# Attention block on one core: values' halves set between contexts and scores, the scores' second part set behind the next query half, and round-trip turns at the attention's end no longer tied to the last norm

## The chip, the cores and the metric

The kernel runs on one core of a Trainium2 chip. A core has five engines with instruction streams of their own: TensorE (PE in the profile; its weight loads are listed as PEld), VectorE (DVE), ScalarE (ACT), GpSimd (POOL) and SyncE (SP), which issues most transfers. The metric is the device time of one execution in microseconds (us), lower is better; a kernel's time is the median of its runs.

## The reference, cut to what matters

A pre-norm transformer block in float32 on 2048 tokens of width 1024 (the file's shapes, with the batch dimension left out here):

```python
x = x + attention(layernorm(x), wq, bq, wk, bk, wv, bv)
x = x + ffn(layernorm(x), w1, w2, w3)

# attention: 32 heads of 32; each token attends over its own heads
q, k, v = (h @ w.T + b).reshape(S, 32, 32)
scores  = einsum("shd,std->sht", q, k) / sqrt(32)
context = einsum("sht,std->shd", softmax(scores), v)

# ffn: the weights go through a 4-bit rounding and back (NF4, blocks of 64)
h = silu(x @ dq(w1).T) * (x @ dq(w2).T)
y = h @ dq(w3).T
```

The attention mixes the heads of one token, not tokens, so it falls into 2048 tiny 32x32 products. `dq` is the weights' round trip: divide a block by its largest magnitude, round to one of 16 levels, multiply back.

## The kernel before

**Tiles.** The 2048 tokens are 16 tiles of 128 (`NT = 16`). All of it stands in `forward`; what follows is its fast half (`if fast:`), which is the one that runs. PE takes its instructions in the order in which the program writes them (`manual_schedule` for TensorE). The other engines' orders are made by the framework's scheduler from the dependences, so a piece of work that is written late can be placed early on DVE, ACT, POOL or SP, if nothing holds it back.

**One tile of attention** passes through these helpers (lines of the kernel before):

- `prepare(i)` normalises the tile's input `xt` into `xn` on ACT and POOL (L592, L579, L585). `split(i)` transposes `xn` on PE (L618) and writes a high part `xh` on ACT (L620) and a low part `xl` on DVE (L621).
- `Q(i, n)`, `K(i, n)`, `V(i, n)`, each for a half n = 0, 1 of the output columns: 16 matmuls of 128x128 by 128x512 into one PSUM bank `pj` (`project`, L648), then a transposing copy out of the bank on DVE (L665 into `qd` or `kd`, L678 into `vd`), with the bias after the second half.
- `S(i, part)`: the scores of half of the tile's tokens, 64 products of 32x32 (L696; the trace shows them as 128 matmuls and 128 weight loads) into the buffer `at`. After part 1 comes the softmax: maximum (L733), subtraction (L735), `Exp` on ACT (L741), a transpose into `prT` (L743).
- `G(i, part)`: the contexts, again 64 tiny products (L700) from `prT` and `vd` into `at`. After part 1 DVE divides by the sums (L758, L760 into `pw`), transposes (L768), adds the residual (L771), SP stores the result and loads the input of tile i + 3, and ACT and POOL normalise it (`norm`, L578 to L585).
- `keep(i)` transposes the normalised result on PE (L511), copies it out on ACT (L512) and stores it for the FFN, with sums and differences made on DVE (L527).

**Buffers that order the work.** `at` takes four of the eight PSUM banks and exists once: scores and contexts take turns in it, so `S(i, 0)` must wait until `G(i-1, 1)` has been read by `pw` (L760). The other four banks turn among `pj`, the transposes `pt` and the weights' transposes `ptw`. `qd`, `kd`, `vd`, `prT` and `xn` have one buffer each.

**The round trip.** The FFN's weights are rounded in the background by a generator. `advance(n)` grants it n * 10/17 turns; a turn is one rounding band (an ACT activation L299 and a DVE step L303 or L305), or the maxima of the next chunk. `flush(1)` writes one half of a finished chunk's transposes to PE (L219), which ACT copies out (L220). Where `held["behind"]` is set, `turn()` tells the scheduler to place the turn's instructions behind the instruction named there.

**The order of one turn of the loop** over tiles i = 3 to 14, before: Q(i,0), Q(i,1), keep(i-2), K(i,0), G(i-1,0), K(i,1), G(i-1,1), V(i,0), S(i,0), V(i,1), split(i+1), S(i,1). Tile 2 has a shorter turn, and tile 15 has no split. In front of the loop stand V(1,0), S(1,0), V(1,1), S(1,1), K(2,1), keep(0), split(3).

**The end of the attention.** After the loop, `plain_block` gives the first eight quads of FFN matmuls (four 128x512 products each, 3.6 us a quad in the trace) in pieces; keep(14), G(15,0), G(15,1) and keep(15) stand between the pieces. After G(15,1) the kernel sets `held["behind"]` to the last instruction of tile 15's norm, and it stays set through the FFN. The first unit of the FFN (`Unit.first`, `Unit.middle`) copies its first product out on ACT (L1416) before PE may go on accumulating in that bank.

Of the kernel before, what the change touches and what calls it, by code (L numbers as in the profile page):

```python
# [21 lines left out]
S = 2048  # L22
# [8 lines left out]
NT = S // P  # L31
# [99 lines left out]
def forward(ctx, tc, const, fast, x, wqT, wkT, wvT, qb, kb, vb, w1, w2, w3, out):  # L131
# [20 lines left out]
    hook = {"scale": "ACT"}  # L152
# [92 lines left out]
    def flush(steps=3):  # L245
        for _ in range(steps):
            if pending and next(pending[0], flush) is flush:
                pending.pop(0)
# [194 lines left out]
    def load_op(name, tbp):  # L443
        tag = "T1" if name == "B12" else name
        t = wpool.tile([P, 4, TB], FP, tag=tag, name=f"x{name}")
        nc.sync.dma_start(t, xd[name, tbp])
        ops[tag] = (name, tbp, t)
# [83 lines left out]
    if fast:  # L531
# [108 lines left out]
                for n in range(2):  # L640
                    take(n, ps[i, n])

        def project(m, i, n, take):

            ps = bank("pj")
            for k in range(KC):
                for part in xs[i]:
                    nc.tensor.matmul(  # L648
                        ps,
                        part[:, k, :],  # L650
                        W[m][k // 2][:, k % 2, ts(n, TB)],
                        start=k == 0 and part is xs[i][0],
                        stop=k == KC - 1 and part is xs[i][1],
                        skip_group_check=True,
                    )
            take(n, ps)
            advance(1)

# [44 lines left out]

        qd, kd, prT, ats = {}, {}, {}, {}

        def Q(i, n):
            if not n:
                qd[i] = qk("q", i, qb_sb)
            project("q", i, n, qd[i][1])

        def K(i, n):
            if not n:
                kd[i] = qk("k", i, kb_sb)
            project("k", i, n, kd[i][1])

        def V(i, n):
            project("v", i, n, take_v)
            if n:
                del xs[i]

        def S(i, part):

            if not part:
                ats[i] = ps_at.tile([P, 4, 512], FP, tag="at", name="sc")
            at = ats[i]
            score(at, qd[i][0], kd[i][0], part)
            advance(1)
            if not part:
                return
            del qd[i], kd[i], ats[i]  # L730
            sc = at[:, :, 0:256].rearrange("p g (s t) -> p g s t", t=NH)
            mx = small.tile([P, 4, 8], FP, tag="mx", name="mx")
            nc.vector.tensor_reduce(mx, sc, AX.X, ALU.max)  # L733
            pr = work.tile([P, 32, NH], FP, tag="pr", name="pr")
            nc.vector.tensor_tensor(  # L735
                pr.rearrange("p (g s) t -> p g s t", g=4),
                sc,
                mx.unsqueeze(3).to_broadcast([P, 4, 8, NH]),
                ALU.subtract,
            )  # L740
            nc.scalar.activation(pr, pr, AF.Exp, scale=1.0 / math.sqrt(D))  # L741
            prT[i] = work.tile([P, 32, NH], FP, tag="prT", name="prT")
            nc.vector.transpose(prT[i], pr)  # L743
# [37 lines left out]
        def keep(i):  # L781
            keep_T(i, x1n.pop(i))
# [36 lines left out]
        G(0, 1)  # L819
        prepare(3)  # L820
        V(1, 0)
        S(1, 0)
        V(1, 1)
        S(1, 1)
        K(2, 1)
        keep(0)
        split(3)
        for i in range(2, NT):
            last = i == NT - 1
            if i > 2:  # L830
                if not last:
                    prepare(i + 1)
                Q(i, 0)
                Q(i, 1)
                flush(1)
                keep(i - 2)
                K(i, 0)
            if last:
                for name in ("B11", "B21"):
                    load_op(name, 0)  # L840
            G(i - 1, 0)
            if i > 2:
                K(i, 1)
            flush(1)
            G(i - 1, 1)
            if last:
                until("2", 0)
                w0 = []
                for n, tag in enumerate(("xh", "xl")):
                    t = work.tile([P, 2, 4, P], FP, tag=tag, name="w0", bufs=2)  # L850
                    nc.sync.dma_start(t, wd["2", 0][:, 2 * n : 2 * n + 2])
                    w0 += [t[:, 0], t[:, 1]]
                for name in ("B12", "B22"):
                    load_op(name, 0)
            V(i, 0)
            S(i, 0)
            V(i, 1)
            flush(1)
            if not last and i > 2:
                split(i + 1)  # L860
            S(i, 1)
            advance(2)
        hook["scale"] = "both"
        left.close()
# [10 lines left out]
        hook["pool"] = (ps_tail, "pj", 2)  # L875

        plain = plain_block(w0, 0)
        next(plain)
        advance(1)
        next(plain)  # L880
        keep(NT - 2)
        advance(1)
        next(plain)
        G(NT - 1, 0)
        next(plain)
        G(NT - 1, 1)
        held["behind"] = hook["normed"]
        for _ in range(3):
            next(plain)
            advance(2)  # L890
        keep(NT - 1)
        hs = {0: next(plain)}
        advance(2)
        sweep.close()
        sweep_at.close()
        right.close()
# [3 lines left out]
    else:  # L900
# [196 lines left out]
        last = t3  # L1097
# [605 lines left out]
```

## Time and profile before

| what | value |
|---|---|
| median of 3 runs | 2229.97 us (2224.99 to 2238.79) |
| the profiled execution, time | 2238.77 us |
| its span, first to last instruction | 2236.9 us |
| PE busy | 2167.1 us (97%) |
| DVE busy, ACT busy | 1378.0 us (62%), 1287.2 us (58%) |
| mean granted clock of TensorE | 0.984 of full |
| the tiles' loop, from V(2,0) to the end of S(15,1) | 107.1 to 580.5 us |
| from there to the FFN's steady run | 580.5 to about 660 us |
| the FFN's steady run | about 660 us to the end |

Busy time is the union of an engine's instructions. The waits view lists idle time of an engine by the instruction that ended it; "issue" there means that the engine waited for nothing that the profile shows. In the timeline a row gives start, length, line, operation, tile, number of instructions, and in square brackets the idle time ahead of it and what ended that.

### The profile page before, as it was taken

How to read it: one execution, taken by the hardware profiler on the slowest of the kernel's cores; microseconds unless marked ns; L12 is line 12 of the kernel's file. 1: busy time of each engine (PE TensorE's matmuls, PEld its weight loads, DVE VectorE, ACT ScalarE, POOL GpSimd, SP SyncE). 2: the span in 40 equal slices, each digit the busy share in tenths (PEclk: the TensorE clock that was granted, in tenths of full speed). 3: DMA queues.
4: the chain of work that ended last, by engine and by line, in shares of the span. 5: the costliest groups of instructions: out<-in, count | busy, mean ns of one | idle time of the engine just before them, and what ended most of it. 6: DMA issues, size and time to landing. Idle time of an engine off the chain costs nothing.

```text
span 2236.9 us, 35174 instructions
## 1 busy us (share of the span) xinstructions
PE 2167.1 (97%) x14193; PEld 1173.4 (52%) x14193; DVE 1378.0 (62%) x1600; ACT 1287.2 (58%) x2529; POOL 302.2 (14%) x425
## 2 busy tenths in 40 slices
PE   7999999989989999999999999999999999999998
PEld 6777787778534444444444444444444444444432
DVE  6778777786377565576565665756666656653022
ACT  7566665662285756758657666676586575511200
POOL 2010010100001203104012021040130210401300
PEclk9899999999999999999999999999999999999999
DMA  8132323234558837579349596394883776974972
GB/s 292 40 101 93 117 65 115 95 98 144 216 193 294 172 141 180 163 280 252 137 141 210 206 283 149 124 214 162 308 207 133 181 190 224 269 236 136 255 290 96
DMA packets 154683, 402.72 MB, mean 180 GB/s; under 512 B 13648, under 2 KB 67920, under 8 KB 137360
## 3 DMA queue, kind: packets, MB, share of 16 engines
q1 hardware_dynamic: 113808, 326.92, 40.7%
q0 software_dynamic: 40704, 73.47, 19.7%
q8 instruction: 113, 1.85, 0.3%
q14 instruction: 58, 0.48, 0.1%
HBM read 227.07 MB, written 173.28 MB: 179 GB/s over the span
## 4 chain that ended last, share of the span: by engine, by line
PE 48%; issue 14%; DMA 5%; DVE 2%; ACT 2%; POOL 1%; DVEq 0%; POOLq 0%; ACTq 0%; SPq 0%
PE z L391 18%; PE q L391 8%; PE z L1511 8%; PE rr L391 4%; PE y L1511 4%; DMA wd<-wop 3%; DMA x1d<-acc 3%; PE r L1511 2%; PE po L1594 1%; PE ptw L219 1%; DVE r L305 1%; PE po L1605 1%; ACT wn L259 1%; POOL x1d L1526 1%; ACT acc L1524 0%
## 5 line engine op out<-in xcount | busy, mean ns | idle before, releaser
L299 ACT ACTIVATE sg<-wn 128x1024 int8<-128x1024 f32 (+1 forms) x520 | 542.5, 1052 | 138.6 <-DVE r L305 128.0
L305 DVE CUSTOM_DVE_ANT_0 r<-r,sg 128x1024 f32<-128x1024 f32 (+1 forms) x455 | 551.4, 1212 | 31.1 <-ACT sg L299 12.0
L1526 POOL DMA_DIRECT2D x1d<-acc x280 | 244.8, 900 | 1253.2 <-ACT acc L1524 1220.0
L391 PE MATMUL z<-xB,w 128*128 128x512 f32 x720 | 320.9, 595 | 3.5 <-ACT u L1430 2.1
L391 PE MATMUL z<-xT,w 128*128 128x512 f32 x656 | 297.5, 596 | 8.3 <-ACT g L1416 8.2
L391 PE MATMUL q<-xT,w 128*128 128x512 f32 x656 | 291.1, 592 | 0.0
L1511 PE MATMUL z<-w,h 128*128 128x512 f32 x496 | 230.5, 593 | 1.7 <-ACT acc L1524 1.5
L391 PEld LDWEIGHTS z<-xB,w 128*128 128x128 f32 x720 | 135.0, 191 | 163.5 <-issue 157.1
L259 ACT ACTIVATE wn<-wn,rc 128x64 f32<-128x64 f32 x736 | 189.0, 340 | 40.2 <-DVE rc L279 40.1
L391 PEld LDWEIGHTS z<-xT,w 128*128 128x128 f32 x656 | 124.1, 192 | 159.7 <-issue 149.0
L391 PEld LDWEIGHTS q<-xT,w 128*128 128x128 f32 x656 | 123.1, 190 | 148.4 <-issue 146.3
L303 DVE TENSOR_SCALAR r<-sg 128x1024 f32<-128x1024 int8 (+1 forms) x65 | 44.5, 684 | 194.7 <-PE ptw L219 194.4
L1511 PEld LDWEIGHTS z<-w,h 128*128 128x128 f32 x496 | 92.6, 190 | 112.7 <-issue 102.8
L1511 PE MATMUL y<-w,h 128*128 128x512 f32 x320 | 148.8, 592 | 0.0
L391 PE MATMUL rr<-xB,w 128*128 128x512 f32 x328 | 147.5, 592 | 0.0
L220 ACT COPY wop<-ptw 128x512 f32<-128x512 f32 (+1 forms) x130 | 76.2, 586 | 113.2 <-PE ptw L219 87.7
L1524 ACT COPY acc<-z 128x512 f32<-128x512 f32 x160 | 92.6, 581 | 70.7 <-PE z L1511 54.5
L1426 DVE TENSOR_TENSOR g<-g,rr 128x512 f32<-128x512 f32 x41 | 27.9, 681 | 168.4 <-PE rr L391 168.3
L259 ACT ACTIVATE r<-r,am 128x64 f32<-128x64 f32 x440 | 113.0, 343 | 8.9 <-DVE r L305 8.6
L271 DVE TENSOR_REDUCE am<-wn 128x16 f32<-128x1024 f32 (+1 forms) x65 | 78.6, 1209 | 48.0 <-ACT r L259 45.6
L648 PE MATMUL pj<-wv,xh 128*128 128x512 f32 x240 | 105.1, 438 | 1.2 <-issue 1.2
L648 PE MATMUL pj<-wv,xl 128*128 128x512 f32 x240 | 101.0, 421 | 0.0
(144 smaller groups left out, 2730.3 us busy)
## 6 DMA issues: line engine op xcount, KB each, us to landing
x1d<-acc POOLq DMA_DIRECT2D x280, 256.0 KB, 6.8
wd<-wop SPq DMA_DIRECT2D x31, 2048.0 KB, 8.5
w<-wd SPq DMA_DIRECT2D x41, 1280.0 KB, 7.0
wn<-in_w_dram SPq DMA_DIRECT2D x63, 512.0 KB, 6.0
xT<-xdT SPq DMA_DIRECT2D x28, 1024.0 KB, 7.6
xB<-xdB SPq DMA_DIRECT2D x24, 1024.0 KB, 6.7
w<-wd SPq DMA_DIRECT2D x44, 512.0 KB, 4.3
w<-wd SPq DMA_DIRECT2D x10, 1536.0 KB, 8.3
```

Of the source, the lines that this page charges most:

```text
L220: nc.scalar.copy(o[:q, first + half], pt[:q])
L259: nc.scalar.mul(dst[:, ts(n, BLOCK)], src[:, ts(n, BLOCK)], by[:, n : n + 1])
L271: nc.vector.tensor_reduce(am[:, :nb], v.rearrange("p (b e) -> p b e", e=BLOCK), AX.X, ALU.max, apply_absolute_value=True,)
L299: nc.scalar.activation(t, v, AF.Copy, bias=bias, scale=scale)
L303: nc.vector.tensor_scalar(r, t, top, low, ALU.min, ALU.max)
L305: nc.vector._custom_dve(TENSOR_ADD_SAT, out=r, in0=r, in1=t, s0=top, s1=low)
L391: nc.tensor.matmul(dst, w[:, k, :], xop[:, k, :], start=start and k == 0, stop=stop and k == 3, skip_group_check=True,)
L648: nc.tensor.matmul(ps, part[:, k, :], W[m][k // 2][:, k % 2, ts(n, TB)], start=k == 0 and part is xs[i][0], stop=k == KC - 1 and part is x ...
L1426: nc.vector.tensor_tensor(self.g0, self.g0, r, ALU.add)
L1511: nc.tensor.matmul(dst, side[n][:, ts(q, P)], w3T[g[2 * m]][:, W3[n]], start=start and m == 0, stop=stop and m == 1, skip_group_check=True,)
L1524: nc.scalar.copy(t, src)
L1526: nc.gpsimd.dma_start(x1d[8 * tbp + 2 * q + j][n], t, accum_op=ALU.add)
```

## The change

1. In the loop, V(i,0) and V(i,1) both stand between G(i-1,1) and S(i,0). K(i,1) moves ahead of G(i-1,0), so that K's halves are together.
2. S(i,1) moves out of tile i's turn: it is written behind the matmuls of Q(i+1,0), ahead of the copy out of their bank (`project` gets a parameter `first`, called between the matmuls and `take`). For the last tile it stands behind the first FFN piece.
3. split(i+1) moves from behind V(i,1) to the place between G(i-1,0) and G(i-1,1).
4. In front of the loop the order becomes V(1,0), V(1,1), S(1,0), split(3), S(1,1), K(2,1), G(1,0), keep(0), G(1,1).
5. At the end of the attention the pieces, turns and flushes are spread anew (`piece(n)`), keep(15) stands behind the eighth quad instead of the seventh, and `held["behind"]` is not set any more.

```diff
-        def project(m, i, n, take):
+        def project(m, i, n, take, first=lambda: None):
...
+            first()
             take(n, ps)
             advance(1)
...
-        def Q(i, n):
+        def Q(i, n, first=lambda: None):
             if not n:
                 qd[i] = qk("q", i, qb_sb)
-            project("q", i, n, qd[i][1])
+            project("q", i, n, qd[i][1], first)
...
         V(1, 0)
+        V(1, 1)
         S(1, 0)
-        V(1, 1)
+        split(3)
         S(1, 1)
         K(2, 1)
+        G(1, 0)
         keep(0)
-        split(3)
+        G(1, 1)
         for i in range(2, NT):
             last = i == NT - 1
             if i > 2:
                 if not last:
                     prepare(i + 1)
-                Q(i, 0)
+                Q(i, 0, lambda: S(i - 1, 1))
                 Q(i, 1)
                 flush(1)
                 keep(i - 2)
                 K(i, 0)
-            if last:
-                for name in ("B11", "B21"):
-                    load_op(name, 0)
-            G(i - 1, 0)
-            if i > 2:
                 K(i, 1)
-            flush(1)
-            G(i - 1, 1)
+                flush(1)
+                if last:
+                    for name in ("B11", "B21"):
+                        load_op(name, 0)
+                G(i - 1, 0)
+                if not last:
+                    split(i + 1)
+                G(i - 1, 1)
+            V(i, 0)
...
-            V(i, 0)
-            S(i, 0)
             V(i, 1)
             flush(1)
-            if not last and i > 2:
-                split(i + 1)
-            S(i, 1)
+            S(i, 0)
             advance(2)
...
-        next(plain)
-        advance(1)
-        next(plain)
+        def piece(n):
+            got = next(plain)
+            advance(n)
+            return got
+
+        piece(1)
+        S(NT - 1, 1)
+        piece(2)
         keep(NT - 2)
-        advance(1)
-        next(plain)
+        piece(2)
+        piece(2)
         G(NT - 1, 0)
-        next(plain)
+        piece(2)
+        flush(1)
         G(NT - 1, 1)
-        held["behind"] = hook["normed"]
-        for _ in range(3):
-            next(plain)
-            advance(2)
+        piece(1)
+        flush(1)
+        piece(1)
+        hs = {0: piece(1)}
         keep(NT - 1)
-        hs = {0: next(plain)}
-        advance(2)
```

## Prediction

> **What bounds the kernel now.** I read the page first (busy shares, granted clock, DMA queues), then the waits of PE over the loop, then PE's timeline around each kind of wait.
>
> PE is the bound, but not evenly. From 660 us on it works 1558.7 of 1570 us (busy time by stretches), so nothing but fewer matmuls helps there. Over the loop, 107 to 581 us, PE works 446 of 474 us, and these waits end its idle time:
>
> ```profile
> PE sc L696 <- DVE pw L760: 10.7, 7, 3.0
> PE sc L696 <- issue: 8.1, 6, 2.5
> PE pj L648 <- ACT xh L620: 3.3, 6, 0.8
> PE sc L696 <- DVE rc L278: 2.2, 1, 2.2
> PE pj L648 <- DVE xl L621: 1.5, 6, 0.3
> PE pj L648 <- issue: 1.2, 1, 1.2
> ```
>
> The columns are the sum, the number and the longest in us. Two are what the change aims at: scores that wait for the contexts' buffer (pw, and rc in the same place), and Q that waits for the split. The "issue" rows need a closer look.
>
> ```profile
> 495.78 1.93 PE L696 MATMUL sc<-kd,qd 32*32 32x32 f32 x118 [2.88 <-DVE pw L760]
> 499.19 0.41 PE L696 MATMUL sc<-kd,qd 32*32 32x32 f32 x10 [1.48 <-issue]
> ```
> ```profile
> 101.37 1.99 PE L700 MATMUL cx<-vd,prT 32*32 32x33 f32 x128
> 103.29 1.11 PE L219 MATMUL ptw<-ident,r 128*128 128x128 f32 x4
> 104.33 0.66 PE L700 MATMUL cx<-vd,prT 32*32 32x33 f32 x31
> 105.67 1.55 PE L700 MATMUL cx<-vd,prT 32*32 32x33 f32 x97 [0.68 <-issue]
> ```
> ```profile
> 58.11 2.09 PE L696 MATMUL sc<-kd,qd 32*32 32x32 f32 x128
> 60.12 1.09 PE L618 MATMUL pt<-ident,xn 128*128 128x128 f32 x8
> 61.15 0.55 PE L696 MATMUL sc<-kd,qd 32*32 32x32 f32 x22
> 61.94 1.78 PE L696 MATMUL sc<-kd,qd 32*32 32x32 f32 x106 [0.23 <-issue]
> ```
> ```profile
> q8 instruction: 113, 1.85, 0.3%
> ```
>
> PE runs dry in the middle of a row of tiny products. Queue q8 brings 113 packets; PE and PEld have 28,386 instructions, so a packet holds about 251. Counting matmuls and weight loads in order of start, every "issue" wait in the loop ends at the same place of a period of 256. [...] If a block is used up sooner than the fetch takes, PE waits. A half of contexts or scores is exactly 256 instructions, in 1.22 or 1.96 us from start to start. In the two places where two such halves stood with only a few transposes between them (the last two timeline fences), the time from entering the block to going on was 3.83 us (101.84 to 105.67) and 3.43 us (58.51 to 61.94).
>
> Elsewhere, before the loop and after it:
>
> ```profile
> 99.47 1.97 PE L618 MATMUL pt<-ident,xn 128*128 128x128 f32 x8 [2.98 <-ACT xn L585]
> ```
> ```profile
> 629.95 6.05 PE L391 MATMUL z<-xT,w 128*128 128x512 f32 x8 [8.25 <-ACT g L1416]
> ```
>
> Short waits also cost clock. After the 1.07 us wait at 535.37 us the granted clock is halved, and V runs its 16 matmuls in 5.54 us instead of 4.00:
>
> ```profile
> 535.80:539.10 3.30, 3.30 (x9) 2.53 (x9) 3.27 (x5) 0.96 (x1) 1.13 (x1) 0.50 0.96 388
> ```
>
> **The change, part by part.** No PE work is removed; what counts is waits.
>
> *Contexts' buffer (V's halves together).* Between G(i-1,1) and S(i,0) stood one half of V, 3.93 us (85.73 to 89.66 from block to block); now two stand there, 7.9 us. The longest wait was 3.0, so pw came at most 6.9 us after G. All 12.9 us (10.7 + 2.2) go. DVE runs the same instructions, 26 of 34 us a tile busy, so pw is not late again.
>
> *Split moved between the contexts.* Q(i+1,0) had only S(i,1), 2.0 us, to cover the copies xh and xl; now V, V and S(i,0), 9.9 us. It waited at most 0.8 + 0.3. So 3.3 + 1.5 = 4.8 us go. The split's own input, xn, is ready some 10 us ahead: in the built order ACT makes it before the softmax's Exp of S(i-1,1), and 12 us of Q, keep and K follow.
>
> *Clock behind these waits.* The V blocks at 147.47, 219.47, 355.28, 427.33 and 499.53 us took 5.16, 5.03, 5.33, 5.17 and 6.48 us against 4.00: 7.2 us. Q at 156.73 us took 9.55 against 7.75, less 0.14 of wait inside: 1.66. Together 8.8 us go.
>
> *Issue waits that hung on the buffer.* At 426.73 and 499.19 us (1.91 and 1.48) PE's program was held in front of S, and the packet came only 1.0 and 1.1 us after S began: 3.4 us go. At 535.37 and 567.95 us (1.07, 1.02, and 1.54, 1.55 of slow V) S followed one half of V; with two there are 3.9 us more for the fetch: 5.2 us go. The rest (1.17, 0.17, 2.50 and 1.65 of clock) I leave.
>
> Sum of what goes in the loop: 12.9 + 4.8 + 8.8 + 3.4 + 5.2 = **35.1 us**.
>
> *New: the contexts' halves stand close.* Before, a half of K (3.9 us) lay between G(i-1,0) and G(i-1,1); now it is the split's eight transposes, 0.97 us (1.04 less the overlap). A run of 256 is 240 of contexts and 16 of transposes: 1.14 + 0.97 = 2.1 us. The fetch took 3.6 us (mean of 3.43 and 3.83), so PE waits 1.5 us in the second half of every pair. For tiles 3 to 14 that is 12 x 1.5 = 18; tile 15 has no split between, 3.6 - 1.2 = 2.4. The bounds are in the packets: over the contexts of the loop they started 0.7 to 2.6 us after the block was entered, and PE could go on 2.2 to 2.6 us after the start. So 0.8 to 3.0 us a pair; I take the two rows of the same shape. Clock: a halved stretch lasts 3.4 us and costs 1.7. The waits of 1.0 to 1.2 us at 353, 535 and 568 us, beside scores, were followed by it; the one at 455.64 us, 1.17 behind contexts and ahead of V, was not. The new wait stands like the last, but is longer: I take one pair in three, 13 x 1.7 / 3 = 7.4; ends 0 and 22.1. Sum **+27.8 us**.
>
> [...]
>
> *Start.* xn(3) hangs on the load of tile 3, issued at 89.12 us when tile 0's residual frees its buffer, and is done at 99.42. The change leaves this chain as it is, but asks earlier: after G(0,1) (79.8) come V, V, S, 9.8 us, so PE stands from 89.6 to 99.4, 9.8 us instead of 3.0. S(1,1), K(2,1), G, keep and G then still follow: 2.0 (transposes) + 2.0 + 3.9 + 1.3 + 1.0 + 1.2 = 11.4; G waits some 2 us for prT (K's copy out stands ahead of it on DVE) and 1.5 for the block. V(2,0) starts at about 114.3 instead of 107.1, with a ptw (0.5) left for later: **+7 us**, ends 4 and 9.
>
> *End.* Untying the turns lets ACT and DVE round weights between 500 and 600 us, where ACT was nearly idle, instead of all at once after 608 us. So the 8.25 us wait for g, and 2.45 of clock (6.05 against 3.60), go: -10.7. But the built order now puts three bands (1.22 each on DVE) between the sums and the residual of tile 15, and on ACT two bands and ten scalings (2 x 1.04 + 10 x 0.25, less 1.0 of POOL time that was there) between its square and its last norm. Before, that norm ended at 608.74, 1.2 us ahead of its transposes. Now keep(15) waits 3.7 + 3.6 - 1.2 = 6.1, with 1.7 of clock behind it: +7.8. Sum **-2.9 us**, ends -10.7 and +3 (the g wait partly stays). SP's queue issues the same transfers, with one weight load earlier; nobody waits on it there. In the FFN's run all waits sum to 10.5 us; I take 0, ends -3 and +3.
>
> **Sum:** -35.1 + 27.8 + 7 - 2.9 = **-3.2 us** against the profiled execution (2238.8 to 2235.6). That execution is the slowest of the three runs, 8.8 us over the median; from the median, 2229.97, the forecast is **2227 us**. All good ends together (all issue and clock losses of the loop gone, 0.8 us a pair without clock) give about -39 (2191), all bad ones (3.0 us a pair with clock, the 5.2 us kept) about +47 (2277).
>
> **Rivals.** (a) *The fetch is hidden*, PE's queue being filled ahead during K: at 0 a pair, -35.1 + 7 - 2.9 = -31, 2199 us. For it: after K the packet sometimes starts before the block is reached. Against: both rows of this shape show the wait. (b) *Slower: the fetch takes longer and each wait halves the clock.* Packets at the first halves of the loop often started 2.2 us late; 2.2 + 2.4 = 4.6, a wait of 2.5, with 1.7 of clock: 13 x 4.2 = 54.6, so -35.1 + 54.6 + 7 - 2.9 = +23.6, 2254 us. It decides from (35.1 + 2.9 - 7) / 13 = 2.4 us a pair; my forecast has 2.1. (c) *The buffer wait stays*, since DVE's order puts rounding bands ahead of pw: 12.9 and most of the clock (6) back, +16, 2246 us. Against: 7.9 us of cover over a worst case of 6.9.
>
> **How the numbers follow.** Forecast 0.58 (own range 2214 to 2241), (a) 0.17, (b) 0.15, (c) 0.10. The range of 8 in 10 is 2203 to 2251. About 1% (22 us) is what a measurement of this kernel can tell from no change. Below 2207.7 lies most of (a) and a little of the forecast: 0.17. Above 2252.3 lies most of (b) and a little of (c): 0.15. Between: 0.68.
>
> **What would show it.** Right: no pw, xh or xl waits of PE in the loop; "issue" waits at cx, one a tile, 1 to 2 us; about 10 us before split(3)'s transposes; no 8 us wait for g, but one of some 6 us at keep(15)'s transposes. Wrong: cx without waits, or the scores waiting for pw again, or new waits in the FFN's run.

## The result, and the profile after

The changed kernel takes 2269.53 us (median, 2262.05 to 2270.16), the kernel before 2235.11 us beside it: a ratio of **1.0153 [1.0128, 1.0178]**, 1.5% slower. In a second set of runs it came to 1.0136 [1.0112, 1.0160]. The forecast was 2227 us with 2203 to 2251 as its range of 8 in 10; 2269.53 lies above it.

The profiled executions compare as 2269.34 us (span 2267.5) to 2238.77 us (span 2236.9), 30.6 us. By the starts of the same instructions in both traces this splits into four stages (`rr` is a tile of FFN products):

| stage | before | after | difference | forecast |
|---|---|---|---|---|
| up to V(2,0) | 107.1 | 115.1 | +8.0 | +7 |
| V(2,0) to the end of S(15,1), without the FFN piece (3.7 us) that now stands ahead of it | 473.3 | 490.6 | +17.3 | -7.3 |
| from there to the first `rr` of the FFN, that piece added back | 55.4 | 51.9 | -3.5 | -2.9 |
| first `rr` to the end | 1601.1 | 1610.0 | +8.9 | 0 |

In the loop (107 to 590 us), the waits view of PE has lost the rows that the change aimed at: the scores wait neither for `pw` nor for `rc`, and Q waits neither for `xh` nor for `xl`. Before, the waits of the loop added up to 27.6 us (the six rows of the forecast, and 0.6 for `wop`); now they are 47.7, 2.9 of them at G(1), ahead of V(2,0). The columns are sum, number and longest, in us.

```profile
PE cx L701 <- issue: 28.6, 13, 5.7
PE pj L648 <- DVE qd L666: 6.4, 3, 4.0
PE pj L648 <- ACT wop L220: 6.3, 3, 2.6
PE cx L701 <- DVE prT L744: 2.5, 2, 2.0
PE pt L511 <- ACT cx L585: 2.2, 2, 1.4
```

Three things are to be seen. The first row is the fetch wait of the forecast, 28.6 us with G(1)'s and 27.8 without, instead of 20.4. Its instructions are counted in the trace: queue q8 (`instruction`) brought 113 packets, 1.85 MB, while PE and PEld had 28,386 matmuls and weight loads, 251 to a packet, and in order of start the 13 waits of this row end at one place of a period of 256, which slips by 38 from the first wait to the last, 16,346 instructions later. Such a period is a block here. The second and third are new: K waits for something that the forecast never named, PSUM banks that are still to be copied out into `qd` and `wop` (before, 0.6 us). The small ones below show DVE and ACT late in other places, too.

The clock is not what was lost. The windows view over the loop gives the granted clock as the figure behind PEld, DVE, ACT and POOL: 0.96 before, 0.97 after in these two windows, and 0.97 in both when they are cut to the loop's own ends. First before, then after:

```profile
107.00:581.00 474.00, 446.19 (x8489) 363.92 (x8481) 364.88 (x406) 262.36 (x528) 42.12 (x104) 0.96 0.34 112
```
```profile
107.00:610.00 503.00, 453.88 (x8757) 369.99 (x8756) 369.52 (x416) 279.57 (x573) 60.84 (x104) 0.97 0.34 111
```

The fetch wait in PE's timeline, once with the usual length and once with a late block:

```profile
366.37 0.97 PE L701 MATMUL cx<-vd,prT 32*32 32x33 f32 x90
372.54 0.77 PE L701 MATMUL cx<-vd,prT 32*32 32x33 f32 x38 [5.19 <-issue]
...
479.01 1.29 PE L701 MATMUL cx<-vd,prT 32*32 32x33 f32 x128
480.24 1.09 PE L618 MATMUL pt<-ident,xn 128*128 128x128 f32 x8
481.26 1.21 PE L701 MATMUL cx<-vd,prT 32*32 32x33 f32 x118
483.45 0.31 PE L701 MATMUL cx<-vd,prT 32*32 32x33 f32 x10 [0.99 <-issue]
```

At 479 us the picture is the one that the forecast drew: a block is entered at 480.08 and used up 2.4 us later, and PE stands for 1 us. At 372 us the packet of the next block began only 5.1 us after its predecessor was entered (most of the others have 0.8 to 1.9), and PE stood for 5.19 us. Three more pairs are like it.

What the late packets have in common is other traffic. In the windows view the last three figures are the clock, the busy share of the 16 DMA engines and GB/s. First the stretch from the entry of the block to the start of that late packet, then the same stretch of a pair with an early one:

```profile
364.96:370.10 5.14, 2.38 (x152) 2.06 (x139) 5.14 (x6) 4.10 (x5) 0.00 (x0) 1.00 0.92 315
```
```profile
405.28:406.57 1.29, 1.29 (x56) 1.15 (x42) 1.29 (x3) 1.29 (x7) 0.00 (x0) 1.00 0.06 13
```

In the four late pairs this share is 0.80 to 0.97. Over ten profiles with close halves of contexts, the contexts waited for 26 packets that began 2.9 us or more behind the entry, and in all 26 cases other transfers filled at least 79% of the engines' time until then; where nothing else moved, the packet began at most 1.6 us behind it. Some packets were early in spite of traffic (1.1 and 1.5 us after the entry at 144.19 and 331.08 us, at a share of 0.96 and 0.91), and no run moved a transfer, so this goes with the late packets and is not shown to cause them.

The new wait of K, in PE's rows and in DVE's:

```profile
463.87 1.04 PE L511 MATMUL pt<-ident,cx 128*128 128x128 f32 x8
468.89 0.76 PE L648 MATMUL pj<-wk,xh 128*128 128x512 f32 x1 [3.98 <-DVE qd L666]
```
```profile
464.51 2.48 DVE L305 CUSTOM_DVE_ANT_0 r<-r,sg 128x1024 f32<-128x1024 f32 x2
466.90 1.22 DVE L734 TENSOR_REDUCE mx<-sc 128x32 f32<-128x1024 f32 x1
468.04 0.71 DVE L666 STREAM_TRANSPOSE qd<-pj 128x512 f32<-128x512 f32 x1
468.67 1.19 DVE L736 TENSOR_TENSOR pr<-sc,mx 128x1024 f32<-128x1024 f32 x1
469.77 0.70 DVE L666 STREAM_TRANSPOSE qd<-pj 128x512 f32<-128x512 f32 x1
```

Four PSUM banks turn among `pj`, `pt` and `ptw`. Q's halves and keep's two groups of transposes take one each, so K's first half needs the bank of Q's first half. Its products end at 458 us, but DVE rounds weights (L305), then takes the scores' maximum, which now stands ahead of Q's copy, and copies Q out at 468.04. K starts right after. Where a group `ptw` stands between, K starts when ACT's copy out of that group ends (at 172.73 and 291.08 us), and the wait is listed under `wop`.

The start and the end in PE's timeline:

```profile
99.54 1.97 PE L618 MATMUL pt<-ident,xn 128*128 128x128 f32 x8 [7.92 <-ACT xn L585]
...
644.35 1.97 PE L511 MATMUL pt<-ident,cx 128*128 128x128 f32 x8 [6.56 <-ACT cx L585]
```

split(3) ends at the same time as before (99.47 there), only PE stands in front of it for 7.92 instead of 2.98 us. At the end the 8.25 us wait for `g` is gone and keep(15) waits 6.56 us for the last norm; 6.1 was forecast.

In the FFN's run (from 660 us) the second and the third of these rows are new:

```profile
PE z L1517 <- ACT acc L1530: 3.7, 6, 1.1
PE z L391 <- DMA w<-wd: 3.3, 1, 3.3
PE ptw L219 <- ACT wop L220: 2.9, 2, 2.2
```

PE waits at 2028 us for weights that come from the round trip. A stretch of half clock (0.50 for 3.41 us) follows it, as behind two waits of 2.2 us, at 790 us for `u` and at 1055 us for `wop`. From the first `rr` to the end PE is idle or past its last matmul for 23.5 us instead of 18.2, and busy for 1586.4 instead of 1582.8; that is the 8.9.

### The profile page after: what moved, and what is told of

Its sections match the earlier page's. It is cut to its first block, busy times and chain, and to the rows that moved or that the text cites. A ratio compares the mean times of both kernels' runs of the same rounds, so it can differ in the third digit from the quotient of the medians.

```text
span 2267.5 us, 35201 instructions
## 1 busy us (share of the span) xinstructions
PE 2167.0 (96%) x14193; PEld 1174.6 (52%) x14193; DVE 1369.9 (60%) x1599; ACT 1287.8 (57%) x2545; POOL 323.3 (14%) x425
## 3 DMA queue, kind: packets, MB, share of 16 engines
q8 instruction: 113, 1.85, 0.3%
## 4 chain that ended last, share of the span: by engine, by line
PE 49%; issue 26%; DVE 8%; ACT 7%; DMA 6%; POOL 4%; SPq 0%; POOLq 0%; DVEq 0%; ACTq 0%
PE z L391 15%; PE z L1517 7%; PE q L391 7%; PE pj L648 6%; DMA x1d<-acc 4%; PE y L1517 4%; PE rr L391 3%; DVE r L305 2%; PE r L1517 2%; POOL x1d L1532 1%; PE po L1600 1%; PE ptw L219 1%; DVE cx L769 1%; PE cx L701 1%; PE sc L697 1%
## 5 line engine op out<-in xcount | busy, mean ns | idle before, releaser
L305 DVE CUSTOM_DVE_ANT_0 r<-r,sg 128x1024 f32<-128x1024 f32 (+1 forms) x455 | 553.2, 1216 | 22.7 <-ACT sg L299 3.3
L648 PE MATMUL pj<-wk,xh 128*128 128x512 f32 x224 | 94.3, 421 | 12.7 <-DVE qd L666 6.4
```

What stands on the lines that cost most here:

```text
L305: nc.vector._custom_dve(TENSOR_ADD_SAT, out=r, in0=r, in1=t, s0=top, s1=low)
L648: nc.tensor.matmul(ps, part[:, k, :], W[m][k // 2][:, k % 2, ts(n, TB)], start=k == 0 and part is xs[i][0], stop=k == KC - 1 and part is x ...
```

## The experiments

The theory after the result: the loop lost by fetch waits and by waits for the turning banks, the start lost by split(3), the FFN's run by something at the attention's end. The rivals: the untying does it all, since it lets ACT and DVE round weights in the loop; or the issue waits at the contexts are not the fetch. All ratios are to the kernel before, run on the same chip beside it, with 95% intervals. "The FFN's run" is from the first `rr` to the end of the span. A loop's time is from V(2,0) to the end of S(15,1); where S(15,1) stands behind the first FFN piece (the changed kernel and all made from it) that piece's 3.7 us are in it, so the changed kernel has 494.3 and before 473.3.

**e1_start.** The changed kernel with the start of before.

```diff
         V(1, 0)
-        V(1, 1)
         S(1, 0)
-        split(3)
+        V(1, 1)
         S(1, 1)
         K(2, 1)
-        G(1, 0)
         keep(0)
+        split(3)
+        G(1, 0)
+        flush(1)
         G(1, 1)
```

> The changed kernel with the order of before at its start alone (V(1,0), S(1,0), V(1,1), S(1,1), K(2,1), keep(0), split(3), then G(1,0) and G(1,1)). Theory: the early split(3) costs what the two traces differ by at V(2,0), 115.10 against 107.14 us, so 7 to 8 us are gained (2261 to 2263 us when the changed kernel takes 2269.5) and the wait of 7.92 us for xn at L618 falls to about 3. Rival: tile 3's load is the limit whatever the order is, and the wait moves on into the loop: within 2 us of the changed kernel.

Measured: 2247.0 us, 1.0033 [1.0011, 1.0055]. V(2,0) starts at 106.14 us instead of 115.10, so the start was worth 9.0. But the kernel gained more: the loop's waits for banks fell from 12.7 to 2.1 us as well, with nothing in the loop edited. The start also decides in which tile each group `ptw` falls and where the scheduler puts the rounding, and the bank waits hang on these. That is a reading; which of the two places matters was not tried. The size expected was wrong, in the loop; the fetch waits stayed (26.1 us).

**e2_kbetween.** The changed kernel with K's second half between the contexts again, the split between V's halves.

```diff
                 K(i, 0)
-                K(i, 1)
                 flush(1)
...
                 G(i - 1, 0)
-                if not last:
-                    split(i + 1)
+                K(i, 1)
                 G(i - 1, 1)
             V(i, 0)
+            if i > 2 and not last:
+                split(i + 1)
```

> The changed kernel with K's second half between the two contexts' halves again, and the split between the two halves of V. Theory: the contexts' issue waits (28.6 us in the loop) go, since 3.9 us of K lie between two blocks that are used up in 1.2 us each, and with them 4 to 10 us of halved clock; the waits of K for its PSUM bank shrink too, because K's second half comes later. 28 to 40 us gained: 2230 to 2242 us. Rival 1: the wait is not the fetch but the vd or prT of the contexts, and stays: within 5 us of the changed kernel. Rival 2: the split moved behind V makes Q of the next tile wait for xh and xl again (some 5 us), so that only 23 to 35 us are gained.

Measured: 2264.61 us, 1.0113 [1.0090, 1.0136], far less than the 28 us or more expected. The fetch waits went as the theory had it, 28.6 to 1.2 us (G(1)'s, ahead of the loop). About half of that was given back in the loop, to banks above all (12.7 to 22.0 us); the loop takes 479.4 us instead of 494.3. Most of these 14.9 us were lost outside it: V(2,0) starts 2.3 us later, and the FFN's run takes 1618.2 us instead of 1610.0. Waits of PE from 107 to 590 us:

```profile
PE pj L648 <- ACT wop L220: 14.4, 3, 6.1
PE pj L648 <- DVE qd L666: 7.6, 2, 4.3
PE cx L701 <- DVE prT L744: 4.6, 3, 2.0
PE pj L648 <- issue: 4.3, 2, 2.5
...
PE cx L701 <- issue: 1.2, 1, 1.2
```

K(i,0) for its bank and G for `prT` wait longer. They seem to have one cover in common, the time that PE stands elsewhere: a wait that is removed exposes the next.

**e3_tied.** `held["behind"]` is set again behind G(15,1) in the changed kernel.

> The changed kernel with the turns tied to the last norm again. Theory: the g wait of 8 us at z (L391) is back and the wait of keep(15) for its transposes (6.56 us) shrinks by 4 to 6: 0 to +5 us against the changed kernel (2269 to 2275). The run of the FFN is told apart by this: if the 8.9 us that it lost (three halved stretches and a wait of z for w, none of which before had) come from the untying, they go too and the kernel gains 4 to 9 us (2260 to 2265). If they come from elsewhere, the later waits are those of the changed kernel.

Measured: 2272.27 us, 1.0141 [1.0117, 1.0165], as the changed kernel. The `g` wait is back (6.6 us), the wait of keep(15) is gone, and `w` is late in the FFN's run all the same (4.4 us). So the tie does not decide that.

**e4_vtogether.** The kernel before with V's halves together ahead of S(i,0), alone.

```diff
             V(i, 0)
-            S(i, 0)
             V(i, 1)
+            S(i, 0)
             flush(1)
```

> The kernel before with one part of the change alone: V's two halves together ahead of S(i,0), the split then between the two halves of the scores; the contexts keep K between them. Theory: the waits for pw and rc (12.9 us) and the halved clock behind them (5 to 9) go, and a fetch wait of 0.5 to 1 us a tile comes between the two halves of scores, which stand with 1 us of transposes between (3.4 us from block to block in the one such place before, against 1.96 + 0.97): -6 to -17 us against before. Rival: the buffer waits only move into S(i,1), which now comes 4 us sooner after S(i,0): within 5 us of before.

Measured: 2236.59 us, 0.9988 [0.9974, 1.0001]: no more than a trace of a gain. The `pw` and `rc` waits are gone, but between the two halves of scores the fetch wait is 11.3 us in 10 waits, and the split, with nothing but scores behind it, makes Q wait 10.6 us for `xh` and `xl` (4.8 before). The fetch was in the theory's price, the split's longer wait was not.

**e5_double.** The changed kernel with the split's transposes made twice from tile 4 on.

```diff
-                for k in range(4):
-                    nc.tensor.transpose(pt[:, k, :], src[:, ts(4 * half + k, P)], ident)
+                for k in range(4 if i < 4 else 8):
+                    nc.tensor.transpose(pt[:, k % 4, :], src[:, ts(4 * half + k % 4, P)], ident)
```

> The changed kernel with the split's eight transposes made twice from tile 4 on (the same result is written into the same place again): 8 more transposes, 0.97 us more PE work, between the two contexts' halves of eleven tiles (10.7 us in all). Theory (PE's program comes in blocks of 256 instructions, and PE waits for the next one in the second half of the contexts): the work fits into the wait, and also moves the block's edges, 16 instructions a tile: the wait of 28.6 us shrinks by 8 to 12 and the time is within 5 us of the changed kernel. Rival (the wait is for data that comes later by as much, or for the contexts' own operands): 10 to 13 us slower than the changed kernel.

Measured: 2256.04 us, 1.0070 [1.0040, 1.0099]. With 10.7 us more work on PE the kernel is faster than the changed one, by more than either side expected. The fetch wait fell by 15.9 us, more than the work that was put into it; a wait for data that come at a time of their own would have shrunk by that work at most:

```profile
PE cx L701 <- issue: 12.7, 11, 4.5
PE cx L701 <- DVE prT L744: 2.8, 2, 2.0
PE sc L697 <- issue: 2.5, 3, 1.2
PE pj L648 <- issue: 1.3, 1, 1.3
PE pj L648 <- ACT wop L220: 0.9, 1, 0.9
```

The bank waits went, too (12.7 to 0.9), and the FFN's run grew to 1617.7 us. The rounding stands in other places on DVE and ACT in this kernel; the time is therefore no clean price of the transposes, only the fetch row speaks.

**e6_keepearly.** The changed kernel with keep between Q's halves.

```diff
                 Q(i, 0, lambda: S(i - 1, 1))
+                keep(i - 2)
                 Q(i, 1)
                 flush(1)
-                keep(i - 2)
```

> The changed kernel with keep(i-2) between Q's two halves instead of behind them. Theory: K waits for one of the four PSUM banks that pj, pt and ptw take in turn, because Q's second half is copied out late (DVE still has the softmax of the scores that now stand behind Q's first half); with keep between, four more products of other work lie between Q's copies and K, so the waits K <- qd and K <- wop (12.7 us in the loop) go, and some halved clock with them: 10 to 16 us gained on the changed kernel (2253 to 2260 where it takes 2270). Rival: the banks only come round elsewhere (Q's second half or the contexts' norm waits instead), within 4 us of the changed kernel.

Measured: 2255.75 us, 1.0070 [1.0046, 1.0095], 0.7 to 0.8% less than the changed kernel, about the gain expected. There is no wait for `qd` or `wop` in the loop any more. In their place stand 4.2 us of keep for its norm and 3.9 us for a bank that keep's copies `xT` hold; the fetch row is 20.0.

**e7_untied.** The kernel before without the tie.

> The kernel before with one part of the change alone: the turns at its end are not tied to the last norm. Theory: the g wait of 8.25 us and the halved clock behind it go and keep(15) waits longer: -5 to +1 us, with an FFN run as before (1601 us from the first rr, and no wait for w). Rival: the untying is what costs the FFN's run its 9 to 18 us: then w is late near 2000 us here too, and the kernel is 5 to 12 us slower than before.

Measured: 2232.68 us, 0.9966 [0.9951, 0.9981]. The `g` wait shrinks from 8.25 to 4.1 us, keep(15) does not wait, the FFN's run is 1602.0 us and has no wait for `w`. Untying alone is a small gain; it is not what the kernel lost by.

**e9_comb.** The changed kernel with e1, e2 and e6 together: the start of before, K between the contexts, the split between V's halves, keep between Q's halves.

> The changed kernel with three parts put back or moved: the start of before, K's second half between the contexts' halves (split between V's), and keep between Q's halves. What stays of the change: V's halves together ahead of the scores, the last scores behind Q's first half, the untied end. Theory: no fetch wait at the contexts, few waits for banks, loop idle of 10 us or less (before 27.8, changed 46.3, the two single edits 30.6 and 33.6): loop 460 to 466 us and, with the FFN's run of 1618 us that the other two showed, 2228 to 2240 us. Rival: each cover that is put back exposes the next wait (as K between did with the banks): 2245 to 2255.

Measured: 2232.66 us, 0.9967 [0.9947, 0.9988]. The loop takes 459.3 us, 14 less than before although the FFN piece is in it, and the granted clock from 107 to 565 us is 0.99 (0.97 before). The FFN's run takes 1614.8 us, with `w` late by 4.0, and eats 13.7 us of what loop, start and end gained (21.8).

**e10_combtail.** The same with the end of before (turns, flushes, tie); the last scores stay behind the first piece.

```diff
-        piece(1)
+        next(plain)
+        advance(1)
         S(NT - 1, 1)
...
+        held["behind"] = hook["normed"]
+        for _ in range(3):
+            next(plain)
+            advance(2)
         keep(NT - 1)
+        hs = {0: next(plain)}
+        advance(2)
```

> The same combination, but with the order of turns and the tie at the end as before the change (the last scores stay behind the first piece of the first FFN block). Theory: what the FFN's run lost (9 us in the changed kernel, 17 to 18 in two of the single edits) comes from where the turns at the end stand, so the run is again 1601 to 1605 us, and the end gets back its 8 us wait for g: 2218 to 2230 us. Rival: the loss comes from the loop's order of turns and is the same here: 2236 us or more.

Measured: **2220.08 us, 0.9900 [0.9867, 0.9934]**, faster than both kernels. The FFN's run is 1601.7 us, without a wait for `w`. What is left of PE's waits in its loop:

```profile
PE pt L511 <- ACT cx L585: 5.5, 4, 1.9
PE pj L648 <- ACT xT L512: 4.3, 2, 3.1
PE ptw L219 <- ACT xT L512: 3.4, 3, 1.2
PE cx L701 <- issue: 3.0, 4, 1.2
```

**e11_aftertail.** The changed kernel with this end.

> The changed kernel with the end of before (its turns, its flushes, its tie; the last scores stay behind the first piece). Theory: the FFN's loss comes from the end's turns: the run from the first rr is 1601 to 1603 us instead of 1610, without a wait for w near 2028 us; the end gets 3 to 4 us longer (the g wait of 8 is back, the 6.6 of keep(15) goes), so 2262 to 2268 us where the changed kernel takes 2270. Rival: the FFN's loss comes from the loop: 2272 to 2275 us.

Measured: 2255.06 us, 1.0067 [1.0039, 1.0095]. The FFN's run is 1599.3 us without a wait for `w`; the `g` wait is back at 8.3. More was gained than expected, because the loop, not edited, came to 482.7 us. Up to 540 us DVE and ACT run the same instructions in the same order as in the changed kernel; from there on the scheduler placed the rounding otherwise. The way from V(2,0) to V(13,0), all of it in the same order, takes 397.7 us instead of 401.8, so 7.5 of the 11.6 us lie in the last part.

**e12_comb_untied.** e10 without the tie.

> The combination of the start of before, K between the contexts, keep between Q's halves and the end's turns of before, now without the tie. Theory: the tie was worth 3 to 4 us at the end (before without it was 55.4 to 51.6 us there) and costs the FFN nothing: 2215 to 2219 us where the tied combination takes 2220. Rival: with the last scores moved into the end, the turns that are let free delay keep(15) by as much: 2219 to 2222, with a keep(15) wait of 5 us or more.

Measured: 2219.86 us, 0.9904 [0.9871, 0.9936], the same as e10. The `g` wait halves (8.3 to 4.3) as in e7, but the FFN's run is 1604.1 us and keep waits more (7.3 us). The 3 to 4 us expected cannot be seen.

**e13_tenturns.** The changed kernel with its last two pieces giving no turn: 10 turns at the end instead of 12.

```diff
         flush(1)
-        piece(1)
-        hs = {0: piece(1)}
+        piece(0)
+        hs = {0: piece(0)}
```

> The changed kernel with 10 turns at its end, as before had, instead of 12 (the last two pieces give none); its flushes stay where they are. If the number of turns is what makes w late near 2028 us and costs the FFN's run its 9 us, the run is 1601 to 1604 us and the kernel 6 to 9 us faster than the changed one (2261 to 2264 where it takes 2270). If it is the place of the flushes (each is one group of four transposes and a copy) the wait for w stays and the time is within 2 us of the changed kernel.

Measured: 2256.11 us, 1.0066 [1.0042, 1.0091]. The FFN's run is 1603.3 us and `w` is not waited for; the flushes stand where the change put them. So it is the number of turns. (Turns are counted here by the argument of `advance`, whose unit is 10/17 of a turn of the generator: two more are 1.2 of its turns.) The kernel gained more than the 6 to 9 us expected; its loop took 487.3 us, though DVE, ACT and PE run the same instructions in the same order in it as in the changed kernel.

**after_again, e14_takefirst, e15_comb_take, e16_comb_take_keep.** The changed kernel once more, and three kernels in which Q's copies stand ahead of the scores' maximum (in e15 on top of e12, in e16 with keep behind both halves of Q again).

```diff
-            first()
             take(n, ps)
+            first()
             advance(1)
```

> The changed kernel once more, beside the other three of this call. If the loss belongs to the kernel: 1.3 to 1.7% slower than before (2268 to 2276 us where before takes 2238), with 25 to 31 us of fetch waits at the contexts and 8 to 14 us of waits of K for a bank. If part of the profiled loop was that execution's: 0.7 to 1.2% slower, with the same kinds of waits and some of them shorter.

> The changed kernel with Q's first copies out of PSUM ahead of the scores' maximum on DVE (in the change they stand behind it, since the scores come between Q's products and its copies). Theory: K takes the bank of Q's first half, so its waits for qd (6.4 us in the loop) shrink by 1.2 us each, and those for wop behind them a little: 3 to 8 us gained on the changed kernel. Rival: the copy is late because DVE still rounds weights, whatever order the two stand in: within 3 us of the changed kernel.

> The combination without the tie, and with Q's copies ahead of the maximum. Theory: the scores' softmax starts 0.7 us later, Q's bank comes free 1.2 us earlier: nothing waits for either in this combination (no wait for qd in its loop), so within 3 us of it, 2217 to 2222 us where it took 2220. Rival: the later softmax makes the contexts wait for prT (1.2 us there now): 2 to 6 us slower.

> The same with keep behind both halves of Q again, as in the changed kernel. Theory: the combination's largest waits are now keep's, for the norm (7.3 us) and its copies (6.6); later keep has more cover, and with K between the contexts and the copies ahead of the maximum the bank waits come back with 3 us at most: 6 to 10 us gained, 2210 to 2215. Rival: the bank waits come back as in the kernel with K between alone (22 us): 2225 to 2235.

Measured, in this order: 2272.53 us, 1.0136 [1.0112, 1.0160]; 2267.64 us, 1.0115 [1.0092, 1.0139]; 2223.87 us, 0.9929 [0.9908, 0.9950]; 2234.35 us, 0.9971 [0.9955, 0.9987]. The loss belongs to the kernel: its second profile has the same rows (fetch 29.5, banks 11.1 us). With the exchange, K's wait for `qd` fell from 6.4 to 1.7 us, but `wop` rose from 6.3 to 10.4: the bank behind it, emptied by ACT, is as late. The order of copy and maximum is not the cause of the bank waits. What is left is that DVE and ACT are behind with the rounding, as the rows at 464 us show; no run took the rounding away. e14's gain on the changed kernel (1.0136 to 1.0115) is not clear of noise. e15 gained nothing (the contexts wait 5.4 us for `prT`), and without the early keep (e16) the waits for `prT`, `wop` and `xT` come back, 482.2 us in the loop, as e16's rival had it.

**e17_twelve.** The kernel before with two more turns at its end, nothing else.

```diff
         hs = {0: next(plain)}
-        advance(2)
+        advance(4)
```

> The kernel before with 12 turns at its end instead of 10 (the last one gives four), nothing else. Theory: the number of turns shifts the rounding against the FFN's loads, so w is 3 to 5 us late near 1990 to 2005 us, and the run from the first rr grows from 1601 to 1610 to 1620 us: 0.4 to 0.8% slower than before. Rival: it needs the moved loop, too: within 3 us of before.

Measured: 2247.86 us, 1.0045 [1.0029, 1.0062]. The FFN's run is 1612.0 us, and PE's waits in it begin with the row that marks the changed kernel:

```profile
PE z L391 <- DMA w<-wd: 4.3, 1, 4.3
PE z L1511 <- ACT acc L1524: 3.5, 5, 1.5
```

Over all kernels here, the ten profiled executions with 12 turns have an FFN's run of 1610.0 to 1620.9 us (mean 1615.3), all with a wait of 3.3 to 5.1 us for `w`; the ten with 10 turns have 1598.8 to 1608.5 (mean 1602.2), none with that wait. SP's queue shows where it comes from, first before, then e17:

```profile
1976.28 0.32 SPq L238 DMA_DIRECT2D wd<-wop  x1
1976.87 6.16 SPq L326 DMA_DIRECT2D wn<-in_wqT_dram  x4
1983.12 0.38 SPq L458 DMA_DIRECT2D w<-wd  x1
```
```profile
1985.18 0.32 SPq L238 DMA_DIRECT2D wd<-wop  x1
1985.78 8.03 SPq L326 DMA_DIRECT2D wn<-in_wqT_dram  x5
1994.73 2.82 SPq L326 DMA_DIRECT2D wn<-in_wkT_dram  x2
1997.65 0.47 SPq L238 DMA_DIRECT2D wd<-wop  x1
1999.07 0.33 SPq L326 DMA_DIRECT2D wn<-in_wkT_dram  x1
1999.46 0.50 SPq L458 DMA_DIRECT2D w<-wd  x1
```

With 12 turns the write of rounded weights goes out 9 us later, and eight loads and a second write stand between it and the load `w` (before: four loads). PE needed `w` at 2002.5 us (it started at 2006.84 after 4.31 of wait), 3.0 us after the load was issued, and such a load lands 7.2 us after its issue (median of 41).

**e18_kfirst.** The kernel before with K's second half ahead of the contexts, nothing else.

```diff
                 K(i, 0)
+                K(i, 1)
...
             G(i - 1, 0)
-            if i > 2:
-                K(i, 1)
             flush(1)
             G(i - 1, 1)
```

> The kernel before with K's second half ahead of the contexts' first, so that the two halves of contexts stand together with at most a group of four transposes between; nothing else. Theory: PE waits for its next block in the second half of each pair, as long as in the changed kernel and the split's 0.97 us more: 2.4 (3.6 less 1.2) to 3.2 us a pair, 29 to 41 us of issue waits at the contexts in 13 pairs, 1.3 to 2.0% slower than before; the waits for pw stay. Rival: the fetch wait came with the moved scores, not with the close halves: 0 to 5 us of issue waits there, within 8 us of before.

Measured: 2261.08 us, 1.0101 [1.0072, 1.0130], less than the 1.3% expected, though the waits are there:

```profile
PE cx L700 <- issue: 30.9, 11, 5.8
PE sc L696 <- issue: 10.6, 4, 4.1
...
PE sc L696 <- DVE pw L760: 1.4, 1, 1.4
```

Close halves alone bring 30.9 us of fetch waits. The waits for `pw` did not stay (10.7 us before), so the net loss is smaller than expected; that DVE catches up while PE stands is the likely reason, not a tested one.

## Why the prediction was wrong, step by step

- **What goes in the loop: right.** `pw`, `rc`, `xh` and `xl` are gone (12.9 and 4.8 us), and of the issue waits at scores and `pj` 9.3 became 1.7, a little more than the 5.5 of waits that the forecast let go. But e4 shows that V's move does not do it alone: with V alone moved, the waits at the scores' fetch and for the split grow from 12.9 to 21.9 us.
- **Contexts' halves close together: mechanism right, size too small.** 20.4 us of fetch waits were forecast for 13 pairs, 27.8 came; e18, which does this alone, has 30.9 (G(1) included). The forecast took the mean of two rows, 3.43 and 3.83 us from entering a block to going on. Nine of the thirteen pairs wait 0 to 1.6 us, as it said; four wait 3.0 to 5.7, because the next packet began 2.9 to 5.1 us after the block was entered, each time with the DMA engines busy. The 3.0 us named as the upper bound for a pair held for the packets seen before the change, not for the fetch. Rival (b) saw this side. PE went on 2.2 to 2.7 us after a packet that began in the block right before the wait; that this packet holds the next block is read from this order and not shown by itself. e2 (K between: no such wait in the loop) and e5 (more work between: 12.7 us) show that it is the fetch.
- **Clock: too good by 3.3 us, and not by the fetch.** 11.9 us less of it (8.8 and 3.1) and 7.4 more were forecast, -4.5 net; what the loop's difference leaves beside the waits (17.3 less 18.5, the idle time 27.8 before and 46.3 after) is -1.2. The stretches of half clock of before are all gone, and six new ones stand in the loop (granted clock 0.50; two of 3.41 us and four of 6.83, where the nine that began in the loop before had 3.41 but for one of 6.83). Four are at the late fetches (3.0 to 5.7 us) and lengthen V by 6.6 us in sum, so the 7.4 was about right, though "one pair in three" was luck: none of the waits of 0.8 to 1.5 us has one, as that of 1.07 us before had. The other two follow K's waits of 2.6 and 4.0 us for a bank and lengthen K by 4.0.
- **The step that failed: no price for the turning PSUM banks.** "DVE runs the same instructions, 26 of 34 us a tile busy, so pw is not late again" looked at `pw` alone. The scores' last part puts the maximum ahead of Q's copies, K's halves stand together, and DVE and ACT round weights in between. K and V waited 13.3 us for banks (`qd`, `wop`, `kd`), with 4.0 of clock behind it, and contexts, keep and split 3.6 us for `prT`, `cx` and `rc`. The sum of the forecast has no term for either. That is 20.9 of the 24.6 us by which the loop missed; the fetch gives 7.4 of wait less 0.8 of clock, and 3 of small waits went beyond the forecast. e6 removes the bank waits by keep's place; e14 shows that the order of copy and maximum alone does not.
- **Start: right in kind**, +8.0 for +7; e1 gave 9.0. In the nine profiles with the changed start V(2,0) begins at 117.0 us on average (112.6 to 119.1), in the eleven with that of before at 107.5 (104.7 to 110.0): 9.5, a little beyond the forecast's end of 9.
- **End: right**, -3.5 for -2.9, by the two waits named (8.25 gone, 6.56 for 6.1).
- **FFN 0, ends -3 and +3: wrong.** The step "SP's queue issues the same transfers, with one weight load earlier" counted transfers and not the turns that feed them. Two turns more at the end shift the rounding against the loads, and the run loses 8.9 us here (19.8 in the second profile of the changed kernel) and 13.1 between the two groups' means. e13 and e17 show it in both directions; e3 and e7 show that it is not the tie.

Together: 24.6 (loop) + 1.0 (start) - 0.6 (end) + 8.9 (FFN) = 33.9 us, the way from the forecast's -3.2 to the 30.6 measured. What stays open is why the same loop costs 482.7 to 494.3 us in kernels that differ only behind it (changed kernel, e3, e11, e13, and the second run with 492.3). It is not the place of the rounding: DVE, ACT and PE run the loop's instructions in the same order in all of them (in e11 up to 540, in e3 up to 557 us). Even so, the waits for `qd` and `wop` are 12.7, 11.1, 11.6 and 10.4 us in the changed kernel's two profiles, e3 and e11, and 6.0 in e13. So one profile of this loop is good to some 7 us, and a bank wait to a factor of two; the 0 to 2.1 us of e1, e5 and e6 lie below all five. Nor was it tried why two turns more move the write of weights by 9 us.

## What to carry to other kernels

A wait that goes is worth its length only if whoever is next in line was not waiting behind the same cover: before a reorder, list for every moved piece which buffers turn, bank by bank, and when their last readers run, not only for the buffer that the change aims at. Two stretches of many tiny instructions were better apart here: close together they brought 28.6 us of fetch waits in the changed kernel and 30.9 in e18, and with a half of K, 3.9 us of large matmuls, between them 1.2 (e2). Background work that is dealt out in turns is to be counted before and after when the places are spread anew; here two turns more cost 13.1 us on average, more than the start's 9.5. And a row of one profile is to be held against a second profile of the same program before a difference of a few us is explained.

## What the runs showed of the hardware that was not expected

- The fetch of PE's next block of 256 came not only late but unevenly: in the pairs of the changed kernel its packet began 0.8 to 1.9 us after the block was entered in most, and 2.9 to 5.1 us after in four, in which other transfers kept the DMA engines 80 to 97% busy until then. Where PE waited, it went on 2.2 to 2.7 us after the packet began. Kernels that spread the tiny products (e9, e10) ran from 107 to 565 us at a granted clock of 0.99; before and changed kernel have 0.97 there.
- More work can be faster: e5 does 10.7 us more on PE and takes 0.7 to 0.8% less than the changed kernel (1.0070 against 1.0153 and 1.0136). The fetch waits fell by 15.9 us and the bank waits by 11.8, each more than that work; the rounding fell into other places on DVE and ACT.
